# Fixing the order of all engines by hand in a four-layer graph attention kernel

## The chip, the core and the metric

The kernel runs on one core of a Trainium2 chip. The core has a matrix engine (TensorE, PE in the profile), a vector engine (VectorE, DVE), an engine for activation functions (ScalarE, ACT), a general engine that here issues the indirect transfers (GpSimd, POOL), an engine that only issues transfers (SyncE, SP), and 16 DMA engines. Each engine works through a list of instructions of its own, and semaphores order the lists among each other. The metric is the time of one execution on the device in microseconds (us); smaller is better.

## The reference

A graph of 3327 nodes with 512 features goes through four attention layers, each with a layer norm and a ReLU ahead of it and a residual around it. The adjacency is sparse: a node has itself and some 16 neighbours. Cut to layer 1 and the frame:

```python
def _L1_gnn_ref(H, A, W, a_l, a_r):
    mask = A + jnp.eye(n, dtype=A.dtype) > 0
    Wh = (H @ W).reshape(n, N_HEADS, D_K)
    sl = jnp.einsum('nhd,hd->nh', Wh, a_l)
    sr = jnp.einsum('nhd,hd->nh', Wh, a_r)
    e = jax.nn.leaky_relu(sl[:, :, None] + sr.T[None, :, :], negative_slope=NEG_SLOPE)
    e = jnp.where(mask[:, None, :], e, -jnp.inf)
    alpha = jnp.nan_to_num(jax.nn.softmax(e, axis=2), nan=0.0)
    out = jnp.einsum('nhm,mhd->nhd', alpha, Wh).reshape(n, OUT_DIM)
    return jax.nn.elu(out)
...
# --- layer 1 (adj_preln) ---
h = jnp.maximum(_layernorm(x, axis=-1), 0.0)
x = x + _L1_gnn_ref(h, adj, L1_gnn_W, L1_gnn_a_l, L1_gnn_a_r)
```

The layers have 8, 4, 1 and 8 heads; layers 1 and 2 end in an ELU, layers 0 and 3 don't. Everything is float32.

## The kernel before

A first stage (the first 416 us of the profile) turns the adjacency into lists of neighbours and projects the input for layer 0. It also sorts the nodes by their number of neighbours, so that each of 26 tiles of 128 nodes has its own cap, from 36 neighbours in tile 0 down to 11 in tile 25, 467 in all. The change leaves this stage as it is.

Then four layers run over the tiles. A table in HBM holds one row of 528 numbers per node: 512 projected features and 16 attention terms. For a tile, POOL gathers the rows of its nodes' neighbours, one indirect transfer of 128 rows per neighbour position, into buffers of four rows each (a group; there are 10 buffers):

```python
CAPS = [36, 25, 23, 22, 21, 21, 20, 20, 19, 19, 18, 18, 17, 17, 17, 16, 16, 15, 15, 15, 14, 14, 13, 13, 12, 11]
GROUP = 4
...
def fetch(l, t):
    groups = []
    for k0 in range(0, CAPS[t], GROUP):
        g = gpool.tile([P, GROUP, ROW], F32, name="g")
        n = min(GROUP, CAPS[t] - k0)
        for q in range(n):
            if l > 0 and k0 + q == 0:
                nc.sync.dma_start(g[:, 0, :], own_d[l % 2][t])
            else:
                gather(g[:, q, :], tabs[l % 2], idx[:, t, k0 + q:k0 + q + 1])
        groups.append((k0, n, g))
        if k0 == GROUP:
            scatter()
    return groups

def scatter():
    while waiting:
        dst, t, rows = waiting.pop(0)
        nc.gpsimd.indirect_dma_start(out=dst, out_offset=bass.IndirectOffsetOnAxis(ap=ids[t], axis=0),
                                     in_=rows, in_offset=None)
```

`attend` computes the weights of each group (z, a leaky step, an Exp), multiplies the rows by them and sums them in PSUM with matmuls by the identity; then it divides by the sum of the weights, applies the ELU where there is one and adds the residual. A float32 matmul shows as two records in the trace.

```python
def attend(l, t, groups):
    ...
    nc.vector.tensor_copy(s[:, :H], groups[0][2][:, 0, F:F + H])
    ...
    for k0, n, g in groups:
        z = small.tile([P, GROUP, 8], F32, name="z")
        nc.vector.tensor_tensor(z[:, :n, :H], g[:, :n, F + 8:F + 8 + H],
                                s[:, :H].unsqueeze(1).to_broadcast([P, n, H]), OP.add)
        nc.vector.scalar_tensor_tensor(z[:, :n, :H], z[:, :n, :H], SLOPE, z[:, :n, :H], OP.mult, OP.max)
        w = wt[:, k0:k0 + n, :H]
        nc.scalar.activation(w, z[:, :n, :H], AF.Exp)
        if H == 1:
            for q in range(n):
                nc.scalar.activation(g[:, q, :F], g[:, q, :F], AF.Copy, scale=wt[:, k0 + q, 0:1])
        else:
            for q in range(n):
                v = g[:, q, :F].rearrange("p (h d) -> p h d", h=H)
                nc.vector.tensor_tensor(v, v, wt[:, k0 + q, :H].unsqueeze(2).to_broadcast([P, H, D]), OP.mult)
        for q in range(n):
            nc.tensor.matmul(po, ident, g[:, q, :F], start=(k0 + q == 0), stop=(k0 + q == K - 1))
    ... # den: sum of the weights, floor, reciprocal
    nc.vector.tensor_tensor(y.rearrange("p (h d) -> p h d", h=H), po.rearrange("p (h d) -> p h d", h=H),
                            den[:, :H].unsqueeze(2).to_broadcast([P, H, D]), OP.mult)
    if ELU[l]:
        elu(y)
    nc.vector.tensor_add(xs[t], xs[t], y)
```

`finish` norms the tile (bn_stats, bn_aggr, nine small steps for the reciprocal root, then xn), and `projected` transposes xn, applies the ReLU, multiplies by the next layer's weights and copies the row v out of PSUM. The row is scattered into the next layer's table by POOL.

```python
def projected(nc, W, xn, ident, ps_t, ps_v, work):
    ...
    for k in range(KC):
        nc.tensor.transpose(pt[:, k, :], xn[:, k * P:(k + 1) * P], ident)
    hT = work.tile([P, KC, P], F32, name="hT")
    nc.scalar.activation(hT, pt, AF.Relu)
    pv = ps_v.tile([P, 2, BANK], F32, name="pv")
    for s in range(2):
        for k in range(KC):
            nc.tensor.matmul(pv[:, s, :HF + H], hT[:, k, :], W.w[:, k, s, :HF + H],
                             start=(k == 0), stop=(k == KC - 1))
    v = work.tile([P, ROW], F32, name="v", bufs=3)
    nc.scalar.activation(v[:, :F].rearrange("p (s n) -> p s n", s=2), pv[:, :, :HF], AF.Copy)
    ...
    nc.vector.tensor_copy(v[:, F:ROW].rearrange("p (s h) -> p s h", s=2)[:, :, :H], pv[:, :, HF:HF + H])
    return v
```

The layers' loop. Only POOL's list is in program order; the lists of the other engines are laid out by the scheduler of the language when the kernel is built.

```python
ctx.enter_context(tc.manual_schedule(engines={mybir.EngineType.Pool}))
for l in range(NL):
    W = Weights(nc, wpool, work, l + 1, ws, avs) if l + 1 < NL else None
    if l == 0:
        gather(xs[0], x, ids[0])
    ahead = fetch(l, 0)
    for t in range(NT):
        if l == 0 and t + 1 < NT:
            gather(xs[t + 1], x, ids[t + 1])
        now, ahead = ahead, fetch(l, t + 1) if t + 1 < NT else None
        attend(l, t, now)
        finish(l, t, W)
    scatter()
```

Of the kernel before, what the change touches and what calls it, by code (L numbers as in the profile page):

```python
# [398 lines left out]
def normed(nc, xt, small, work, half=None):  # L399


    st = small.tile([P, nc.vector.BN_STATS_DIM], F32, name="st")
    nc.vector.bn_stats(st, xt)
    mv = small.tile([P, nc.vector.BN_AGGR_DIM], F32, name="mv")
    nc.vector.bn_aggr(mv, st)
    ve = small.tile([P, 1], F32, name="ve")
    nc.vector.tensor_scalar_add(ve, mv[:, 1:2], EPS)  # L407
    rstd = small.tile([P, 1], F32, name="rstd")
    if half is not None:
        nc.gpsimd.tensor_tensor(rstd, ve, half, OP.pow)  # L410
    else:
        hv = small.tile([P, 1], F32, name="hv")
        nc.vector.tensor_scalar(hv, ve, -0.5, None, OP.mult)
        nc.vector.tensor_scalar(rstd.bitcast(I32), ve.bitcast(I32), -0.5, float(0x5F3759DF), OP.mult, OP.add)
        for _ in range(3):
            q = small.tile([P, 1], F32, name="q")
            nc.vector.tensor_scalar(q, rstd, rstd, hv, OP.mult, OP.mult)
            r2 = small.tile([P, 1], F32, name="rstd")
            nc.vector.tensor_scalar(r2, q, 1.5, rstd, OP.add, OP.mult)
            rstd = r2  # L420
    xn = work.tile([P, xt.shape[1]], F32, name="xn")
    nc.vector.tensor_scalar(xn, xt, mv[:, 0:1], rstd, OP.subtract, OP.mult)  # L422
    return xn


def projected(nc, W, xn, ident, ps_t, ps_v, work):

    F = xn.shape[1]
    HF, KC, H = F // 2, F // P, W.H
    pt = ps_t.tile([P, KC, P], F32, name="pt")  # L430
    for k in range(KC):
        nc.tensor.transpose(pt[:, k, :], xn[:, k * P:(k + 1) * P], ident)  # L432
    hT = work.tile([P, KC, P], F32, name="hT")
    nc.scalar.activation(hT, pt, AF.Relu)  # L434
    pv = ps_v.tile([P, 2, BANK], F32, name="pv")
    for s in range(2):
        for k in range(KC):
# [4 lines that stand above are left out]
    if H < 8:  # L442
        nc.vector.memset(v[:, F:ROW], 0.0)
    nc.vector.tensor_copy(v[:, F:ROW].rearrange("p (s h) -> p s h", s=2)[:, :, :H], pv[:, :, HF:HF + H])  # L444
    return v
# [3 lines left out]
def tile_gat_stack(ctx: ExitStack, tc: tile.TileContext, x, adj, adjT, ws, avs, out):  # L449
# [33 lines left out]
    with ExitStack() as c1:  # L483
# [26 lines left out]
        for t in range(NT):  # L510
            a = apool.tile([P, NP], I32, name="a")
            nc.sync.dma_start(a, adj[t * P:(t + 1) * P, :])
            key = apool.tile([P, NP], F32, name="key")
            nc.vector.scalar_tensor_tensor(key, a, 0.0, keys, OP.is_gt, OP.mult, accum_out=total[:, t:t + 1])  # L514
            dg = key[:, t * P:(t + 1) * P]
            nc.vector.tensor_add(dg, dg, boost)
            cand = small.tile([P, SEGS * 8], F32, name="cand")
            for g in range(SEGS):
                nc.vector.max(cand[:, g * 8:(g + 1) * 8], key[:, g * SEG:(g + 1) * SEG])  # L519
            for r in range(0, KMAX, 8):  # L520
                nc.vector.max(top[:, t, r:r + 8], cand)
# [4 lines left out]
            v = projected(nc, W, normed(nc, xt, small, work, half), ident, ps_t, ps_v, work)  # L526
            nc.sync.dma_start(tabs_v[0][t][t * P:(t + 1) * P, :], v)


# [94 lines left out]
def tile_gat_lists(ctx: ExitStack, tc: tile.TileContext, x, ws, avs, out, ident, half, idx, tabs, tabs_v):  # L624
# [37 lines left out]
                else:  # L662
                    gather(g[:, q, :], tabs[l % 2], idx[:, t, k0 + q:k0 + q + 1])
            groups.append((k0, n, g))
            if k0 == GROUP:
                scatter()
        return groups

# [3 lines left out]
            nc.gpsimd.indirect_dma_start(out=dst, out_offset=bass.IndirectOffsetOnAxis(ap=ids[t], axis=0),  # L672
                                         in_=rows, in_offset=None)

    def elu(y):

        neg = work.tile([P, F], F32, name="neg", bufs=1)
        nc.vector.tensor_scalar_min(neg, y, 0.0)
        th = work.tile([P, F], F32, name="th", bufs=1)
        nc.scalar.activation(th, neg, AF.Tanh, scale=0.5)  # L680
        nc.scalar.activation(neg, neg, AF.Exp)
        nc.vector.scalar_tensor_tensor(th, neg, 1.0, th, OP.add, OP.mult)
        nc.vector.scalar_tensor_tensor(y, y, 0.0, th, OP.max, OP.add)

    def attend(l, t, groups):
        H, D, K = HEADS[l], F // HEADS[l], CAPS[t]
        s = small.tile([P, 8], F32, name="s")
        nc.vector.tensor_copy(s[:, :H], groups[0][2][:, 0, F:F + H])
        wt = spool.tile([P, KMAX, 8], F32, name="wt")
        po = ps_o.tile([P, BANK], F32, name="po")  # L690
        for k0, n, g in groups:
            z = small.tile([P, GROUP, 8], F32, name="z")
            nc.vector.tensor_tensor(z[:, :n, :H], g[:, :n, F + 8:F + 8 + H],  # L693
                                    s[:, :H].unsqueeze(1).to_broadcast([P, n, H]), OP.add)
            nc.vector.scalar_tensor_tensor(z[:, :n, :H], z[:, :n, :H], SLOPE, z[:, :n, :H], OP.mult, OP.max)  # L695
            w = wt[:, k0:k0 + n, :H]
            nc.scalar.activation(w, z[:, :n, :H], AF.Exp)  # L697
            if H == 1:
                for q in range(n):
                    nc.scalar.activation(g[:, q, :F], g[:, q, :F], AF.Copy, scale=wt[:, k0 + q, 0:1])  # L700
            else:
                for q in range(n):
                    v = g[:, q, :F].rearrange("p (h d) -> p h d", h=H)
                    nc.vector.tensor_tensor(v, v, wt[:, k0 + q, :H].unsqueeze(2).to_broadcast([P, H, D]), OP.mult)  # L704
            for q in range(n):
                nc.tensor.matmul(po, ident, g[:, q, :F], start=(k0 + q == 0), stop=(k0 + q == K - 1))  # L706
        den = small.tile([P, 8], F32, name="den")
        nc.vector.tensor_reduce(den[:, :H], wt[:, :K, :H].rearrange("p k h -> p h k"), AX.X, OP.add)  # L708
        nc.vector.tensor_scalar_max(den[:, :H], den[:, :H], TINY)
        nc.vector.reciprocal(den[:, :H], den[:, :H])  # L710
        y = work.tile([P, F], F32, name="y")
        nc.vector.tensor_tensor(y.rearrange("p (h d) -> p h d", h=H), po.rearrange("p (h d) -> p h d", h=H),  # L712
                                den[:, :H].unsqueeze(2).to_broadcast([P, H, D]), OP.mult)
        if ELU[l]:
            elu(y)
        nc.vector.tensor_add(xs[t], xs[t], y)  # L716

    def finish(l, t, W):
        if W is None:
            waiting.append((out_v[t], t, xs[t]))  # L720
            return
        v = projected(nc, W, normed(nc, xs[t], small, work), ident, ps_t, ps_v, work)
        nc.sync.dma_start(own_d[(l + 1) % 2][t], v)
        waiting.append((tabs_v[(l + 1) % 2][t], t, v))

    out_v = dram_disjoint_views(out, NT)
    ctx.enter_context(tc.manual_schedule(engines={mybir.EngineType.Pool}))
    for l in range(NL):
        W = Weights(nc, wpool, work, l + 1, ws, avs) if l + 1 < NL else None
        if l == 0:  # L730
            gather(xs[0], x, ids[0])
        ahead = fetch(l, 0)
        for t in range(NT):
            if l == 0 and t + 1 < NT:
                gather(xs[t + 1], x, ids[t + 1])
            now, ahead = ahead, fetch(l, t + 1) if t + 1 < NT else None
            attend(l, t, now)
            finish(l, t, W)
        scatter()


# [38 lines left out]
```

## Time and profile before

| | |
|---|---|
| time, median of 3 | 3412.91 us (3411.35 to 3419.31) |
| span of the profiled execution | 3598.4 us |
| PE busy | 2458.3 us, 68% |
| DVE busy | 1895.9 us, 53% |
| ACT busy | 585.1 us, 16% |
| POOL busy | 1989.1 us, 55% |
| gathers g<-tab (L647, POOL) | 1790, mean 999 ns |
| sums po<-g,ident (L706, PE) | 3736 records, mean 652 ns |
| products g<-g,wt (L704, DVE; L700, ACT in layer 2) | 1401 of mean 689 ns; 467 of mean 710 ns |
| mean DMA rate | 175 GB/s |

The profiled execution is longer than the timed ones; stages and waits are read from the profile, the result from the times. A line of a group names line, engine, operation and tiles; then come the busy time and the mean of one, and after the bar the idle time of the engine just before these instructions, with what ended it. A line of waits names who waited for whom, with the total, the number of times and the longest. A line of a timeline has start, duration, engine, line, operation, tiles and shapes, and in brackets the idle time ahead of it and what ended it. PEclk is the share of the TensorE clock that was granted.

### The profile page before, as it was taken

The numbers are of one execution on the slowest core, as the hardware profiler recorded it, in microseconds if no ns is written. First come the engines' busy times: TensorE is split into PE (matmuls) and PEld (weight loads), VectorE is DVE, ScalarE is ACT, GpSimd is POOL, SyncE is SP. The second block draws the span as 40 slices with busy tenths as digits, with TensorE's granted clock in tenths as the row PEclk, the third lists the DMA queues.
The fourth block names the chain that finished last, engine by engine and source line by source line (L and its number), as shares of the span: only waits on it lengthen the run. The fifth ranks groups of instructions, "written<-read, shape, count | busy, mean of one in ns | idle before, by whom it ended". The sixth has DMA issues, their size and how long they took to land. (4 is left out here: it accounts for less than half of the span.)

```text
span 3598.4 us, 24474 instructions
## 1 busy us (share of the span) xinstructions
PE 2458.3 (68%) x5830; PEld 1217.5 (34%) x5830; DVE 1895.9 (53%) x5329; ACT 585.1 (16%) x1291; POOL 1989.1 (55%) x2025
## 2 busy tenths in 40 slices
PE   3564076777777657777776757677787857767677
PEld 2443033433334323333333323334343422322222
DVE  8999255555555536556655621222223345555555
ACT  0010000000000001011111134444454400000000
POOL 0002566666666365666655454555555456766666
PEclk8777588888888779889889877788988887879879
DMA  5552466666666475666665465566666556766666
GB/s 198 180 197 90 115 175 172 188 184 181 183 179 179 138 196 165 181 179 189 175 177 163 135 173 156 170 185 172 185 179 186 164 164 185 202 189 196 196 179 180
DMA packets 197001, 628.12 MB, mean 175 GB/s; under 512 B 38482, under 2 KB 42994, under 8 KB 193524
## 3 DMA queue, kind: packets, MB, share of 16 engines
q0 software_dynamic: 154432, 519.29, 51.2%
q1 hardware_dynamic: 33300, 94.07, 8.1%
q10 hardware_dynamic: 9120, 13.11, 1.1%
q8 instruction: 53, 0.87, 0.1%
q14 instruction: 96, 0.79, 0.1%
HBM read 569.76 MB, written 56.57 MB: 174 GB/s over the span
## 5 line engine op out<-in xcount | busy, mean ns | idle before, releaser
L706 PE MATMUL po<-g,ident 128*128 128x512 f32 x3736 | 1877.5, 652 | 547.7 <-issue 239.4
L647 POOL DMA_INDIRECT g<-tab,idx x1790 | 1788.8, 999 | 595.1 <-issue 510.2
L706 PEld LDWEIGHTS po<-g,ident 128*128 128x128 f32 x3736 | 750.0, 207 | 1541.3 <-issue 1078.4
L704 DVE TENSOR_TENSOR g<-g,wt 128x512 f32<-128x512 f32 x1401 | 903.6, 689 | 95.4 <-issue 63.7
L693 DVE TENSOR_TENSOR z<-g,s 128x32 f32<-128x32 f32 (+5 forms) x508 | 91.7, 182 | 969.9 <-DMA g<-tab,idx 903.2
L438 PE MATMUL pv<-w,hT 128*128 128x264 f32 (+2 forms) x1664 | 514.6, 476 | 76.2 <-ACT hT L434 56.8
L438 PEld LDWEIGHTS pv<-w,hT 128*128 128x128 f32 x1664 | 401.0, 245 | 239.5 <-ACT hT L434 91.1
L697 ACT ACTIVATE wt<-z 128x32 f32<-128x32 f32 (+5 forms) x508 | 107.2, 217 | 2122.8 <-DVE z L695 969.9
L432 PE MATMUL pt<-ident,xn 128*128 128x128 f32 x416 | 98.9, 382 | 447.5 <-DVE xn L422 232.5
L672 POOL DMA_INDIRECT tab<-v,idx x78 | 85.7, 1098 | 569.6 <-DVE v L444 501.7
L700 ACT ACTIVATE g<-g,wt 128x512 f32<-128x512 f32 x467 | 302.5, 710 | 3.8
L432 PEld LDWEIGHTS pt<-ident,xn 128*128 128x128 f32 x416 | 65.8, 192 | 528.4 <-issue 243.3
L410 POOL TENSOR_TENSOR rstd<-ve,half 128x1 f32<-128x1 f32 x26 | 14.3, 549 | 309.8 <-DVE ve L407 302.0
L712 DVE TENSOR_TENSOR y<-po,den 128x512 f32<-128x512 f32 x104 | 71.2, 685 | 173.6 <-PE po L706 126.9
L695 DVE SCALAR_TENSOR_TENSOR z<-z 128x32 f32<-128x32 f32 (+5 forms) x508 | 88.0, 178 | 96.1 <-remote 43.6
L519 DVE MAX8 cand<-key 128x8 f32<-128x208 f32 x416 | 129.1, 373 | 0.0
L434 ACT ACTIVATE hT<-pt 128x512 f32<-128x512 f32 x104 | 61.7, 594 | 306.9 <-PE pt L432 136.3
L441 ACT ACTIVATE v<-pv 128x512 f32<-128x512 f32 x104 | 61.4, 590 | 303.1 <-PE pv L438 254.0
L444 DVE COPY v<-pv 128x16 f32<-128x16 f32 (+2 forms) x104 | 17.8, 171 | 147.0 <-ACT v L441 147.0
L514 DVE SCALAR_TENSOR_TENSOR key<-a,keys 128x3328 f32<-128x3328 int32 x26 | 94.0, 3616 | 0.0
L716 DVE TENSOR_TENSOR x<-x,y 128x512 f32<-128x512 f32 x104 | 71.7, 690 | 3.0 <-DVE den L708 1.2
L672 POOL DMA_INDIRECT out<-x,idx x26 | 28.4, 1093 | 77.2 <-DVE x L716 42.0
(83 smaller groups left out, 794.3 us busy)
## 6 DMA issues: line engine op xcount, KB each, us to landing
a<-in_adj SPq DMA_DIRECT2D x26, 1664.0 KB
g<-tab,idx POOLq DMA_INDIRECT x1790
own<-v SPq DMA_DIRECT2D x78, 264.0 KB
g<-own SPq DMA_DIRECT2D x78, 264.0 KB
tab<-v SPq DMA_DIRECT2D x26, 264.0 KB
xt<-in_x ACTq DMA_DIRECT2D x26, 256.0 KB
w<-in_w ACTq DMA_DIRECT2D x8, 512.0 KB
av<-in_a ACTq DMA_DIRECT2D x8, 256.0 KB
```

Source lines behind the costliest of these rows:

```text
L432: nc.tensor.transpose(pt[:, k, :], xn[:, k * P:(k + 1) * P], ident)
L438: nc.tensor.matmul(pv[:, s, :HF + H], hT[:, k, :], W.w[:, k, s, :HF + H], start=(k == 0), stop=(k == KC - 1))
L514: nc.vector.scalar_tensor_tensor(key, a, 0.0, keys, OP.is_gt, OP.mult, accum_out=total[:, t:t + 1])
L519: nc.vector.max(cand[:, g * 8:(g + 1) * 8], key[:, g * SEG:(g + 1) * SEG])
L647: nc.gpsimd.indirect_dma_start(out=out_, out_offset=None, in_=table, in_offset=bass.IndirectOffsetOnAxis(ap=which, axis=0))
L672: nc.gpsimd.indirect_dma_start(out=dst, out_offset=bass.IndirectOffsetOnAxis(ap=ids[t], axis=0), in_=rows, in_offset=None)
L693: nc.vector.tensor_tensor(z[:, :n, :H], g[:, :n, F + 8:F + 8 + H], s[:, :H].unsqueeze(1).to_broadcast([P, n, H]), OP.add)
L695: nc.vector.scalar_tensor_tensor(z[:, :n, :H], z[:, :n, :H], SLOPE, z[:, :n, :H], OP.mult, OP.max)
L697: nc.scalar.activation(w, z[:, :n, :H], AF.Exp)
L700: nc.scalar.activation(g[:, q, :F], g[:, q, :F], AF.Copy, scale=wt[:, k0 + q, 0:1])
L704: nc.vector.tensor_tensor(v, v, wt[:, k0 + q, :H].unsqueeze(2).to_broadcast([P, H, D]), OP.mult)
L706: nc.tensor.matmul(po, ident, g[:, q, :F], start=(k0 + q == 0), stop=(k0 + q == K - 1))
```

## The change

The lists of PE, DVE and ACT are put in program order too, and the program is rewritten into pieces, so that the order can be chosen: as soon as a tile's last sums are traced, its end follows (division, residual, norm), and its transposes (`turn`) and its projection (`project`) are set behind the next tile's groups 0 and 1. In the layers with an ELU the residual and norm (`added`) come behind group 0, the transposes behind group 1 and the projection behind group 2. Besides:

- the scatter stands behind the third group of gathers in place of the second;
- in layers with several heads the fourth row of each group is weighted by ScalarE, one instruction a head, in place of VectorE;
- in the layer with one head the division is done by ScalarE;
- the ELU's lower clamp is a Relu on ScalarE;
- the weights of a layer are prepared in the middle of the layer but one before it.

The purpose is that the end of a tile no longer stands behind work of the next tile that waits for gathers. The core of the diff:

```diff
             groups.append((k0, n, g))
-            if k0 == GROUP:
+            if k0 == 2 * GROUP:
                 scatter()
...
+        def group(self, i):
...
             for q in range(n):
+                if H == 1 or q == 3:
+                    for h in range(H):
+                        v = g[:, q, h * D:(h + 1) * D]
+                        nc.scalar.activation(v, v, AF.Copy, scale=wt[:, k0 + q, h:h + 1])
+                else:
                     v = g[:, q, :F].rearrange("p (h d) -> p h d", h=H)
                     nc.vector.tensor_tensor(v, v, wt[:, k0 + q, :H].unsqueeze(2).to_broadcast([P, H, D]), OP.mult)
...
+        def weighted(self):
...
+            if H == 1:
+                nc.scalar.activation(self.y, po, AF.Copy, scale=den[:, 0:1])
+            else:
+                nc.vector.tensor_tensor(self.y.rearrange("p (h d) -> p h d", h=H), ...
+            if ELU[self.l]:
+                nc.scalar.activation(neg, self.y, AF.Relu, scale=-1.0)
+                nc.scalar.activation(self.th, neg, AF.Tanh, scale=-0.5)
+                nc.scalar.activation(self.ex, neg, AF.Exp, scale=-1.0)
+
+        def added(self):
+            y, xt = self.y, xs[self.t]
+            if ELU[self.l]:
+                nc.vector.scalar_tensor_tensor(self.th, self.ex, 1.0, self.th, OP.add, OP.mult)
+                nc.vector.scalar_tensor_tensor(y, y, 0.0, self.th, OP.max, OP.add)
+            nc.vector.tensor_add(xt, xt, y)
+            if self.W is None:
+                waiting.append((out_v[self.t], self.t, xt))
+            else:
+                self.xn = normed(nc, xt, small, work)
...
-    ctx.enter_context(tc.manual_schedule(engines={mybir.EngineType.Pool}))
+    ctx.enter_context(tc.manual_schedule(engines={mybir.EngineType.Pool, mybir.EngineType.PE,
+                                                  mybir.EngineType.DVE, mybir.EngineType.Activation}))
+    following = Weights(nc, wpool, work, 1, ws, avs)
...
+        late = 1 if ELU[l] else 0
+        todo = {}
+        ahead = Tile(l, 0, W)
         for t in range(NT):
...
+            now, ahead = ahead, Tile(l, t + 1, W) if t + 1 < NT else None
+            if t == NT // 2 and l + 2 < NL:
+                following = Weights(nc, wpool, work, l + 2, ws, avs)
+            now.start()
+            for i in range(len(now.groups)):
+                now.group(i)
+                for piece in todo.pop(i, []):
+                    piece()
+            now.weighted()
+            if late:
+                todo = {0: [now.added], 1: [now.turn], 2: [now.project]}
+            else:
+                now.added()
+                todo = {0: [now.turn], 1: [now.project]}
```

`Tile(l, t, W)` calls `fetch`, `start` copies s, `turn` is the first half of the old `projected` and `project` the second, with the store of v and its entry in `waiting`.

More of the change, by code (lines that the diff above doesn't have):

```diff
@@ L423, in normed, with turned @@
     return xn
-def projected(nc, W, xn, ident, ps_t, ps_v, work):
-    F = xn.shape[1]
-    HF, KC, H = F // 2, F // P, W.H
+def turned(nc, xn, ident, ps_t, work):
+    KC = xn.shape[1] // P
     pt = ps_t.tile([P, KC, P], F32, name="pt")
@@ L434, in projected @@
     nc.scalar.activation(hT, pt, AF.Relu)
+    return hT
+def projected(nc, W, hT, ps_v, work):
+    KC, H = hT.shape[1], W.H
+    F = KC * P
+    HF = F // 2
     pv = ps_v.tile([P, 2, BANK], F32, name="pv")
@@ L525, in tile_gat_stack @@
             nc.scalar.dma_start(xt, x[t * P:(t + 1) * P, :])
-            v = projected(nc, W, normed(nc, xt, small, work, half), ident, ps_t, ps_v, work)
+            v = projected(nc, W, turned(nc, normed(nc, xt, small, work, half), ident, ps_t, work), ps_v, work)
             nc.sync.dma_start(tabs_v[0][t][t * P:(t + 1) * P, :], v)
@@ L673, in scatter @@
                                          in_=rows, in_offset=None)
[L675 to L691, printed above, removed]
+    class Tile:
+        def __init__(self, l, t, W):
+            self.l, self.t, self.W = l, t, W
+            self.groups = fetch(l, t)
+        def start(self):
+            H = HEADS[self.l]
+            self.s = small.tile([P, 8], F32, name="s")
+            nc.vector.tensor_copy(self.s[:, :H], self.groups[0][2][:, 0, F:F + H])
+            self.wt = spool.tile([P, KMAX, 8], F32, name="wt")
+            self.po = ps_o.tile([P, BANK], F32, name="po")
+        def group(self, i):
+            H, K, wt = HEADS[self.l], CAPS[self.t], self.wt
+            D = F // H
+            k0, n, g = self.groups[i]
@@ L692, in attend @@
             z = small.tile([P, GROUP, 8], F32, name="z")
             nc.vector.tensor_tensor(z[:, :n, :H], g[:, :n, F + 8:F + 8 + H],
-                                    s[:, :H].unsqueeze(1).to_broadcast([P, n, H]), OP.add)
+                                    self.s[:, :H].unsqueeze(1).to_broadcast([P, n, H]), OP.add)
             nc.vector.scalar_tensor_tensor(z[:, :n, :H], z[:, :n, :H], SLOPE, z[:, :n, :H], OP.mult, OP.max)
-            w = wt[:, k0:k0 + n, :H]
-            nc.scalar.activation(w, z[:, :n, :H], AF.Exp)
@@ L698, in attend @@
[L698 to L702, printed above, removed]
+            nc.scalar.activation(wt[:, k0:k0 + n, :H], z[:, :n, :H], AF.Exp)
+            for q in range(n):
+                if H == 1 or q == 3:
[3 more added lines that the diff above has]
+                else:
@@ L705, in attend @@
             for q in range(n):
[L706 to L724, printed above, removed]
+                nc.tensor.matmul(self.po, ident, g[:, q, :F], start=(k0 + q == 0), stop=(k0 + q == K - 1))
@@ new lines, in weighted @@
+        def weighted(self):
+            H, K, po = HEADS[self.l], CAPS[self.t], self.po
+            D = F // H
+            den = small.tile([P, 8], F32, name="den")
+            nc.vector.tensor_reduce(den[:, :H], self.wt[:, :K, :H].rearrange("p k h -> p h k"), AX.X, OP.add)
+            nc.vector.tensor_scalar_max(den[:, :H], den[:, :H], TINY)
+            nc.vector.reciprocal(den[:, :H], den[:, :H])
+            self.y = work.tile([P, F], F32, name="y")
+            if H == 1:
+                nc.scalar.activation(self.y, po, AF.Copy, scale=den[:, 0:1])
+            else:
+                nc.vector.tensor_tensor(self.y.rearrange("p (h d) -> p h d", h=H),
+                                        po.rearrange("p (h d) -> p h d", h=H),
+                                        den[:, :H].unsqueeze(2).to_broadcast([P, H, D]), OP.mult)
+            if ELU[self.l]:
+                neg = work.tile([P, F], F32, name="neg", bufs=1)
+                nc.scalar.activation(neg, self.y, AF.Relu, scale=-1.0)
+                self.th = work.tile([P, F], F32, name="th", bufs=1)
+                nc.scalar.activation(self.th, neg, AF.Tanh, scale=-0.5)
+                self.ex = work.tile([P, F], F32, name="ex", bufs=1)
+                nc.scalar.activation(self.ex, neg, AF.Exp, scale=-1.0)
@@ new lines, in added, with turn @@
+        def added(self):
[8 more added lines that the diff above has]
+                self.xn = normed(nc, xt, small, work)
+        def turn(self):
+            if self.W is not None:
+                self.hT = turned(nc, self.xn, ident, ps_t, work)
@@ L726, in tile_gat_lists, with project @@
+        def project(self):
+            if self.W is not None:
+                v = projected(nc, self.W, self.hT, ps_v, work)
+                nc.sync.dma_start(own_d[(self.l + 1) % 2][self.t], v)
+                waiting.append((tabs_v[(self.l + 1) % 2][self.t], self.t, v))
     out_v = dram_disjoint_views(out, NT)
-    ctx.enter_context(tc.manual_schedule(engines={mybir.EngineType.Pool}))
+    ctx.enter_context(tc.manual_schedule(engines={mybir.EngineType.Pool, mybir.EngineType.PE,
+                                                  mybir.EngineType.DVE, mybir.EngineType.Activation}))
@@ L728, in tile_gat_lists @@
+    following = Weights(nc, wpool, work, 1, ws, avs)
     for l in range(NL):
-        W = Weights(nc, wpool, work, l + 1, ws, avs) if l + 1 < NL else None
+        W, following = following, None
         if l == 0:
             gather(xs[0], x, ids[0])
-        ahead = fetch(l, 0)
+        late = 1 if ELU[l] else 0
+        todo = {}
+        ahead = Tile(l, 0, W)
         for t in range(NT):
@@ L735, in tile_gat_lists @@
                 gather(xs[t + 1], x, ids[t + 1])
-            now, ahead = ahead, fetch(l, t + 1) if t + 1 < NT else None
-            attend(l, t, now)
-            finish(l, t, W)
+            now, ahead = ahead, Tile(l, t + 1, W) if t + 1 < NT else None
[12 more added lines that the diff above has]
+                todo = {0: [now.turn], 1: [now.project]}
+        for i in sorted(todo):
+            for piece in todo[i]:
+                piece()
         scatter()
```

## The prediction

> **What bounds the kernel now.** I read the table by stage first, with the stages cut at the last scatter of each layer (416 us is the first gather). Its columns are busy time and count by engine, then PEclk, DMA share and GB/s.
>
> ```profile
> 416.00:1257.00 841.00, 595.80 (x1454) 305.55 (x1454) 467.57 (x1269) 56.51 (x179) 535.99 (x518) 0.81 0.63 178
> 1257.00:2090.00 833.00, 597.62 (x1454) 289.41 (x1454) 490.54 (x1336) 86.14 (x231) 477.01 (x468) 0.86 0.60 171
> 2090.00:2900.00 810.00, 593.66 (x1454) 298.49 (x1454) 214.56 (x831) 380.32 (x698) 451.74 (x467) 0.84 0.61 174
> 2900.00:3594.00 694.00, 488.51 (x934) 190.78 (x934) 383.30 (x876) 28.51 (x127) 464.06 (x467) 0.84 0.67 192
> ```
>
> No engine is full in any layer and the DMA stands at 0.60 to 0.67, so a chain of waits sets the pace. The four layers are 3178 us of the 3598; the change leaves the rest alone. Next the waits of POOL, which issues every gather (engine, tile and line; releaser; us, times, longest):
>
> ```profile
> POOL tab L672 <- DVE v L444: 501.7, 65, 21.3
> POOL out L672 <- DVE x L716: 42.0, 6, 9.7
> ```
>
> The timeline of POOL shows what such a wait is. The scatter of a projected tile stands in POOL's queue between gathers, and everything behind it stops:
>
> ```profile
> 1009.84 1.08 POOL L647 DMA_INDIRECT g<-tab,idx  x1 [0.30 <-issue]
> 1011.23 0.95 POOL L647 DMA_INDIRECT g<-tab,idx  x1 [0.30 <-issue]
> 1016.83 1.20 POOL L672 DMA_INDIRECT tab<-v,idx  x1 [4.66 <-DVE v L444]
> 1018.33 0.96 POOL L647 DMA_INDIRECT g<-tab,idx  x1 [0.30 <-issue]
> ```
>
> Adding POOL's idle ahead of scatters by layer gives 149, 207, 212 and 73 us. Without it, a layer costs POOL its pitch, busy 0.96 to 1.03 plus 0.30 of issue: 519 transfers in layer 0 make 690 us, 467 in each other layer 585 to 612. That is the prize: some 640 us of POOL waiting. The question is what the other engines need per tile.
>
> VectorE shows why v is late, in its timeline at the end of layer 0: the statistics of a tile that is ready stand behind a z that waits for gathers (first three lines), while the last tile runs undisturbed (the others).
>
> ```profile
> 1224.05 0.69 DVE L403 BATCH_NORM_STATS2 st<-x 128x6 f32<-128x512 f32 x1
> 1228.28 0.18 DVE L693 TENSOR_TENSOR z<-g,s 128x24 f32<-128x24 f32 x1 [3.54 <-DMA g<-tab,idx]
> 1228.38 0.18 DVE L405 BATCH_NORM_AGGREGATE mv<-st 128x2 f32<-128x6 f32 x1
> ...
> 1241.57 0.69 DVE L712 TENSOR_TENSOR y<-po,den 128x512 f32<-128x512 f32 x1 [0.92 <-PE po L706]
> 1242.30 0.69 DVE L716 TENSOR_TENSOR x<-x,y 128x512 f32<-128x512 f32 x1
> 1243.03 0.69 DVE L403 BATCH_NORM_STATS2 st<-x 128x6 f32<-128x512 f32 x1
> ...
> 1246.09 0.55 DVE L422 TENSOR_SCALAR xn<-x,mv,rstd 128x512 f32<-128x512 f32 x1
> 1246.55 1.28 DVE L393 TENSOR_TENSOR prod<-w,av 128x512 f32<-128x512 f32 x2
> ```
>
> From y's start to the next free slot behind xn are 1246.55 - 1241.57 = **4.98 us**. Before, this chain is spread among the next tile's weighting; it takes 10 to 16 us there, but TensorE has sums to do meanwhile.
>
> **What the Trainium skill says.** "TensorE: Matmul & The Clock Gate", in the section on the 16 sub-arrays (Architectural detail), says that the queues of ScalarE and VectorE are strict first in, first out. The lines above agree: the aggregate starts 0.10 us after the z that stood ahead of it. So an order fixed by hand makes each wait in the list a wait for all that follows. The same page, Part 1 ("What's actually happening"), gives the clock two states, half and full, judged over windows of some 3.4 us. The trace agrees: only 0.5 and 1.0 occur, in stretches of multiples of 3.41 us, and PEclk of 0.81 to 0.86 means that 28 to 38% of the time ran at half. "ScalarE: Activation LUTs" ("What ACT_TABLE_LOAD costs") gives an ACTIVATE 186 ns + 0.833 ns per element, 93 more for a pointer operand, 93 of overlap back to back. The 128x512 copy with a pointer scale works out at 706; the trace has 710.
>
> **Part 1: POOL.** The scatter queued in tile t+1's gathers now belongs to tile t-2, and stands behind 12 gathers in place of 8. Its v is ready a whole tile earlier, so POOL waits no more for it, only for free gather buffers (10 groups). The 149 + 207 + 212 us end as scatter waits, and gathers lie ready ahead of VectorE.
>
> **Part 2: TensorE's own work.** In the timeline 28 sums take 12.18 us, 0.43 each at full clock; a neighbour is two of them, 0.86 us, 467 neighbours a layer: **401 us**. A projection is 16 matmuls at 0.22, 3.5 us, and 4 transposes at 0.21, 0.86 us.
>
> **Part 3: where TensorE now stands still.** The step times between starts, from the timelines: last sum's slot to y 0.2; s, z and the leaky step to Exp 0.2 + 0.2 + 0.23; Exp to the first product 0.26; product to sum 0.75. Together a restart is 1.64 us.
> - Layer 0. VectorE does y, x, statistics and xn at once, before the next tile's s: 0.2 + 4.98 + 1.64 = 6.8 us without a sum.
> - The turn follows group 0. ScalarE's list has hT, which waits for the transposes, ahead of group 1's Exp. Last transpose to hT 0.46, hT to Exp 0.50, then 0.26 + 0.75, less the transpose's own 0.21: 1.8 us idle.
> - The projection follows group 1. ScalarE's v and VectorE's copy of v's tail stand ahead of group 2: 0.42 + 0.61 + 0.1 + 0.2 + 0.22 + 0.26 + 0.75 - 0.22 = 2.3 us idle.
> - Fixed per tile: 6.8 + 0.9 + 1.8 + 3.5 + 2.3 = 15.3 us. Layer 0: 401 + 26 x 15.3 = 798 us.
> - Layer 1 (ELU). y is 0.72, then Relu, Tanh and Exp (0.6 + 0.65 + 0.54) stand on ScalarE ahead of the next tile's Exp: idle 3.75. After group 0's products VectorE does two ELU steps, x and the statistics, 5.6 us, ahead of group 1's z: 8.9 us from the first product to group 1's first sum, against 0.75 + 3.43 of summing: 4.7 idle. With the common 8.5: 16.9 per tile, 401 + 439 = 840 us.
> - Layer 2 (one head, weights applied by ScalarE). y is on ScalarE too: idle 3.75; group 1 again waits for the end of x and the statistics: 2.7 idle. 14.9 per tile, 401 + 387 = 788 us.
> - Layer 3 has no projection: idle 3.3 per tile, and 0.86 per neighbour is below POOL's 1.29. POOL sets it: 467 x 1.285 = 600, with start and end 630 us.
>
> ScalarE's eight 128x64 products of the fourth row cost an estimated 0.24 us each by the page named above, 1.9 us, done before TensorE reaches that row: nothing on the path. The three products left to VectorE save it 0.6 us a group, where it isn't the one waited for.
>
> **Part 4: the clock.** A pause of 3.8 to 6.8 us fills most of a window, and group 0 then runs at half: 3.4 us more at most, partly hidden in layer 1 by the 4.7 us stall; the 2.3 us stall drops it again now and then. Before, 28 to 38% of 32 us a tile ran at half, 9 to 12 us, some six tenths of it busy, which lost 2.7 to 3.7 us. I take 3.5, 3.0 and 2.7 in the three layers: 239 us.
>
> **Part 5: the rest.** Weights are made in mid-layer, twice: 8 products and 8 sums at 0.7, and a load that waits for the buffer of the first half, 15 us each, 30. At three layer changes the last projection, scatter and first gathers stand alone, some 13 us more each, and the start fills in 10: 50 us.
>
> **Sum:** 798 + 840 + 788 + 630 + 239 + 50 + 30 = 3375 us against 3178: +197. Without the profiler the kernel takes 3413, not 3598; I keep the difference: 3610. The loss by the clock is the softest term, so I go a little below: **3590 us**.
>
> **Rivals.** (a) *POOL becomes the bound*: the waits vanish and layers fall to 690 + 612 + 585 + 600, with 70 for changes: 3413 - 620 = about 2790 us. For it speak the 501.7 us and that these are the longest waits of the gathering engine; against it that the fixed 15 to 17 us per tile exceed what POOL's 1.29 per neighbour leaves above TensorE's 0.86, except for the first tile of 36 neighbours. (b) *The chain is as I drew it, but the clock holds*, since data lies ready and sums run densely between stalls: 239 us less, 3375 - 239 = 3136, so about 3370, no change. (c) *The half clock spreads*: each stall drops it, group 0 and group 1 both run at half, up to 3 us a tile more in three layers, 234 us: 3820. (d) *The profiler slows gathers more than sums*: then the kernel before gains more without it than the one after, worth up to 100 us upward.
>
> **Range and chances.** (b) and the sum mark the lower half, parts of (c) and (d) the upper: 3380 to 3780. Faster by over 2% needs the stalls of part 3 to be hidden by something I don't see: 0.17. Within 2%: 0.15. Slower: 0.68.
>
> **What would show it.** Right: POOL's scatter waits near zero and in their place waits for sums to free buffers; VectorE's 903 us of waiting for gathers gone in the first three layers, replaced by waits for po and for ScalarE; ScalarE waiting for pt and pv with Exp behind; a TensorE pause of some 6.8 us per tile of layer 0; PEclk about 0.8; layer 3 down to about 630 while layers 0 to 2 grow. Wrong: layers 0 to 2 below 750, or POOL busy at its pitch throughout.

## The result and the profile after

The change makes the kernel slower: 3743.43 us (median of 4) against 3412.26 us, a ratio of 1.0966 with a 95% interval of 1.0933 to 1.1000. That is 331 us more.

The same table by stage for the changed kernel, cut again at the last scatter of each layer:

```profile
412.00:1345.00 933.00, 622.74 (x1454) 300.59 (x1454) 439.22 (x1167) 273.29 (x1035) 513.77 (x519) 0.83 0.57 161
1345.00:2279.00 934.00, 629.34 (x1454) 296.79 (x1454) 453.85 (x1202) 235.90 (x685) 463.63 (x467) 0.87 0.54 152
2279.00:3119.00 840.00, 603.94 (x1454) 287.69 (x1454) 195.97 (x774) 413.70 (x750) 450.73 (x468) 0.89 0.59 168
3119.00:3744.00 625.00, 471.07 (x934) 191.56 (x934) 333.22 (x769) 245.11 (x983) 469.48 (x468) 0.90 0.76 213
```

Against the first profile layers 0 and 1 have grown by 92 and 101 us, layer 2 by 30, and the DMA share of layer 1 fell from 0.60 to 0.54: no engine is full, and for the most part the core waits more. TensorE's row of one tile of layer 0, in the timeline, names the waits:

```profile
1001.17 0.60 PE L431 MATMUL pt<-ident,xn 128*128 128x128 f32 x4
1003.30 3.70 PE L715 MATMUL po<-g,ident 128*128 128x512 f32 x8 [1.53 <-DVE g L713]
1006.84 3.67 PE L445 MATMUL pv<-w,hT 128*128 128x260 f32 x16
1012.89 8.83 PE L715 MATMUL po<-g,ident 128*128 128x512 f32 x16 [2.38 <-DVE g L713]
1028.49 6.51 PE L715 MATMUL po<-g,ident 128*128 128x512 f32 x8 [6.77 <-DVE g L713]
1034.84 0.60 PE L431 MATMUL pt<-ident,xn 128*128 128x128 f32 x4
```

In the brackets stand the three pauses of a tile: 1.53 us behind the turn, 2.38 behind the projection, 6.77 behind the last sums. The group after the long pause takes 6.51 us for its eight records, where eight take 3.70 in the second line: most of it ran at half clock. All three pauses end with a product of VectorE, and ScalarE's Exp stands ahead of that product. What the Exp has to wait for differs. Behind the turn it stands behind hT in ScalarE's list, behind the projection behind v; behind the last sums it waits for VectorE, which first works through the tile's end. ScalarE's, POOL's and VectorE's rows show it in the same stretch:

```profile
1001.81 0.60 ACT L433 ACTIVATE hT<-pt 128x512 f32<-128x512 f32 x1 [5.25 <-PE pt L431]
1002.30 0.22 ACT L705 ACTIVATE wt<-z 128x32 f32<-128x32 f32 x1
...
1010.55 0.60 ACT L448 ACTIVATE v<-pv 128x512 f32<-128x512 f32 x1 [5.97 <-PE pv L445]
1011.88 0.23 ACT L705 ACTIVATE wt<-z 128x32 f32<-128x32 f32 x1 [0.73 <-DVE z L704]
...
1035.28 0.95 POOL L654 DMA_INDIRECT g<-tab,idx  x1 [7.00 <-PE po L715]
...
1021.75 0.69 DVE L729 TENSOR_TENSOR y<-po,den 128x512 f32<-128x512 f32 x1 [4.46 <-PE po L715]
...
1026.73 0.27 DVE L692 COPY s<-g 128x8 f32<-128x8 f32 x1
```

ScalarE sat 5.25 us until the transposes were done, with the Exp right behind hT in its list, and 5.97 us until the projection was done, with v ahead of the next Exp. VectorE needs 4.98 us from y to the next tile's s (1026.73 - 1021.75). POOL now waits for sums to free a buffer: in this stretch gathers are not what is short.

### The profile page after: what moved, and what is told of

The parts are those of the page before. It is cut to its first block, busy times and chain, and to the rows that moved or that the text cites. A ratio compares the mean times of both kernels' runs of the same rounds, so it can differ in the third digit from the quotient of the medians.

```text
span 3747.7 us, 27283 instructions
## 1 busy us (share of the span) xinstructions
PE 2507.2 (67%) x5830; PEld 1207.5 (32%) x5830; DVE 1762.4 (47%) x4930; ACT 1201.6 (32%) x3509; POOL 1957.1 (52%) x2025
## 5 line engine op out<-in xcount | busy, mean ns | idle before, releaser
L715 PE MATMUL po<-g,ident 128*128 128x512 f32 x3736 | 2008.0, 694 | 982.4 <-DVE g L713 662.0
L654 POOL DMA_INDIRECT g<-tab,idx x1790 | 1764.5, 986 | 924.2 <-issue 474.6
L715 PEld LDWEIGHTS po<-g,ident 128*128 128x128 f32 x3736 | 794.1, 221 | 2118.2 <-DVE g L713 917.3
L710 ACT ACTIVATE g<-g,wt 128x64 f32<-128x64 f32 (+2 forms) x2607 | 869.1, 411 | 15.4 <-ACT wt L705 0.4
L713 DVE TENSOR_TENSOR g<-g,wt 128x512 f32<-128x512 f32 x1080 | 685.3, 688 | 366.4 <-ACT wt L705 366.4
L445 PE MATMUL pv<-w,hT 128*128 128x264 f32 (+2 forms) x1664 | 447.5, 429 | 21.8 <-ACT hT L433 21.8
L445 PEld LDWEIGHTS pv<-w,hT 128*128 128x128 f32 x1664 | 356.1, 216 | 130.5 <-ACT hT L433 31.9
L431 PE MATMUL pt<-ident,xn 128*128 128x128 f32 x416 | 72.0, 301 | 166.3 <-DVE xn L422 151.3
L745 DVE SCALAR_TENSOR_TENSOR th<-ex,th 128x512 f32<-128x512 f32 x52 | 36.1, 695 | 151.4 <-ACT ex L739 151.4
L735 ACT ACTIVATE neg<-y 128x512 f32<-128x512 f32 x52 | 32.7, 629 | 140.6 <-DVE y L729 139.8
```

The costliest lines, as they stand in the source:

```text
L654: nc.gpsimd.indirect_dma_start(out=out_, out_offset=None, in_=table, in_offset=bass.IndirectOffsetOnAxis(ap=which, axis=0))
L710: nc.scalar.activation(v, v, AF.Copy, scale=wt[:, k0 + q, h:h + 1])
L715: nc.tensor.matmul(self.po, ident, g[:, q, :F], start=(k0 + q == 0), stop=(k0 + q == K - 1))
```

## The experiments

The runs are told in the order of the questions.

### Was the profile of before typical?

`before_again` is the kernel before without an edit.

> The kernel before, unchanged, profiled once more: its profile on hand spans 3598 us though its times are 3411 to 3419. If the profiler stretches this kernel (gathers or their landing), the span is near 3600 again. If that one execution was just long, the span is near 3415, and then the stage lengths of before are some 6% shorter than those the prediction used, and the loss of the change by layer is larger than the two profiles show.

It took 3417.13 us and its profile spans 3415.4. So the profiler does not stretch this kernel; the execution that the first profile shows was a long one. It also has a mark of its own: ScalarE's copy v starts more than 1 us after its matmuls have ended and ScalarE is free in 13 of 104 cases, and in none of before_again. What held it there is not known. The stages of before_again:

```profile
414.00:1226.00 812.00, 582.85 (x1454) 301.75 (x1454) 466.01 (x1268) 56.51 (x179) 534.63 (x519) 0.84 0.65 185
1226.00:2011.00 785.00, 591.20 (x1454) 287.65 (x1454) 490.04 (x1336) 85.37 (x231) 477.90 (x468) 0.89 0.64 181
2011.00:2777.00 766.00, 572.07 (x1454) 289.41 (x1454) 215.35 (x832) 380.34 (x698) 452.01 (x468) 0.87 0.65 184
2777.00:3411.00 634.00, 476.50 (x934) 186.33 (x934) 384.76 (x876) 28.53 (x127) 474.18 (x467) 0.91 0.74 210
```

The layers are 812, 785, 766 and 634 us, 2997 in all, in place of 841, 833, 810 and 694. The loss by layer is thus 121, 149 and 74 us, and 9 us gained in layer 3: 335 together, the measured 331. Of the 344 us lost in the first three layers TensorE is busy for 110 (1746 to 1856 us, the first busy column) and stands still for the other 234.

### Is it the order, or the other parts of the change?

`scheduler_order` is the changed kernel with one line undone:

```diff
-    ctx.enter_context(tc.manual_schedule(engines={mybir.EngineType.Pool, mybir.EngineType.PE,
-                                                  mybir.EngineType.DVE, mybir.EngineType.Activation}))
+    ctx.enter_context(tc.manual_schedule(engines={mybir.EngineType.Pool}))
```

> The changed kernel with only POOL's order fixed; all its other parts (fourth row on ScalarE, division and clamp on ScalarE, scatter behind the third group, weights in mid-layer) stay. Stall theory (the fixed order of PE, DVE and ACT costs the time): close to before or faster, 3200 to 3420 us. Rival (the other parts cost it: eight small products on ScalarE, the weights in mid-layer): near the changed kernel, 3650 to 3750.

3323.58 us, a ratio of 0.9744 (0.9713 to 0.9775) to before. All the parts but the order together are a gain of 84 us against the 3407 us of before, timed beside it; this order by hand alone costs 3743 - 3324 = some 420 us. The rival falls.

`scatter_later_only` takes one of the other parts alone, on the kernel before:

```diff
-            if k0 == GROUP:
+            if k0 == 2 * GROUP:
                 scatter()
```

> The kernel before with only the scatter moved behind the third group of gathers. If POOL's wait for v is what bounds the kernel before, twelve gathers lie ahead of the wait in place of eight, 5 us more for v to come: the wait of 5 to 8 us per tile shrinks or goes, up to 26 x 5 us in three layers, 3050 to 3250 us. If the wait only stands in for a slow v, nothing moves: 3400 +- 30.

3381.72 us, 0.9927 (0.9904 to 0.9950): under 1%, 25 us, far from what the first theory allowed. POOL's wait for v is still 412.9 us in its profile, where it is 428.9 in before_again. The move by itself doesn't free POOL. Why four more gathers ahead of the wait shorten it so little was not taken apart.

### Which of the pauses costs it?

For the next kernels a group was split into its weights and products (`front`) and its sums (`sums`), and the loop sets the fronts of later groups ahead; with AHEAD = 0 it would be the changed kernel.

```diff
+        fronts = [(ahead, i) for i in range(len(ahead.groups))]
...
             for i in range(len(now.groups)):
-                now.group(i)
+                while fronts and (done < j + AHEAD + 1) and (fronts[0][0] is now or fronts[0][0] is ahead):
+                    f, k = fronts.pop(0)
+                    f.front(k)
+                    done += 1
+                now.sums(i)
+                j += 1
                 for piece in todo.pop(i, []):
                     piece()
```

`ahead_inside_tile`: AHEAD = 1, but only fronts of the running tile (`fronts[0][0] is now`).

> The changed kernel with the weights and products of one next group set ahead of the sums, but only within a tile: the turn and the projection no longer hold up the next group's Exp; the pause at the tile's end stays. Stall theory, by its pieces: 1.5 and 2.4 us per tile go in three layers, 26 x 3.9 x 3 = 304 us, and in layer 1 and 2 the wait of group 1 for the added tile shrinks little; 3400 to 3470. If TensorE's pauses at turn and projection were hidden: 3700 and more.

3279.37 us, 0.9620 (0.9604 to 0.9636) of before. That is 464 us less than the changed kernel, more than the 304 that the two pauses were reckoned at. The stages of the first three layers:

```profile
413.00:1203.00 790.00, 574.47 (x1454) 288.81 (x1454) 439.33 (x1167) 273.35 (x1035) 512.82 (x518) 0.85 0.66 190
1203.00:1955.00 752.00, 572.18 (x1454) 281.74 (x1454) 453.12 (x1202) 235.93 (x685) 461.72 (x468) 0.90 0.66 189
1955.00:2652.00 697.00, 569.80 (x1454) 285.05 (x1454) 195.26 (x774) 412.66 (x750) 451.30 (x468) 0.90 0.70 202
```

By layer 143, 182 and 143 us went, 468 in all: TensorE stands still for 328 us less and is busy for 140 us less. The pauses behind turn and projection are gone but for 0.6 us behind the turn in layer 1 and two long waits in the middle of layers 1 and 2; the pause at the end of a tile stands as it was (median 6.67 us in layer 0, 3.5 in layers 1 and 2). The shorter busy time is in the main the clock: TensorE's busy time at half clock fell from 199 + 199 + 146 us to 127 + 100 + 113, and half of that difference, 102 us, is time; what the other 38 are was not taken apart.

`one_group_ahead`: AHEAD = 1 also across the tile's end.

> The same across the tile's end: group 0 of the next tile is weighted ahead of the end. Stall theory: the tile's end now overlaps one group's sums, 3.4 of the 6.8 us of layer 0 and about 3.5 of layers 1 and 2; 26 x 3.5 x 3 = 270 us less than inside the tile alone, 3150 to 3250, most of what two groups ahead bring (3174).

3180.12 us, 0.9327 (0.9311 to 0.9342): another 99 us. Expected were 270. The pause behind the last sums goes in layer 0, and in layers 1 and 2 some 30 pauses with a median of 1.3 us are left between sums; in its place TensorE waits ahead of the transposes for xn, a median of 2.91, 3.20 and 1.26 us per tile in the three layers.

`two_groups_ahead`: AHEAD = 2.

> The changed kernel, order fixed by hand in the same way, but weights and products of the next two groups (also of the next tile's) are set in the lists ahead of a group's sums, so ahead of a tile's end, its turn and its projection. Stall theory: TensorE's three pauses of 6.8, 1.5 and 2.4 us per tile go, TensorE needs some 20.8 us for a tile of 18, POOL 22.7 to 25.2, so POOL's pitch bounds: layers of about 700, 620, 600 and 620 us, 2950 to 3100 in all. Rival (fixed order as such, or the half clock, costs it): 3500 to 3750.

3174.25 us, 0.9317 (0.9297 to 0.9337): better than the kernel before and the changed one, and no different from one group ahead. The expectation of 2950 to 3100 was missed. Its stages, and what TensorE waits for most (the second block; 37.7 us is a wait of the first stage):

```profile
413.00:1125.00 712.00, 560.58 (x1454) 288.16 (x1454) 442.56 (x1167) 271.92 (x1035) 519.11 (x519) 0.90 0.74 211
1125.00:1877.00 752.00, 568.33 (x1454) 291.27 (x1454) 454.17 (x1202) 236.73 (x685) 475.28 (x468) 0.87 0.66 190
```

```profile
PE pt L432 <- DVE xn L423: 480.7, 100, 37.7
PE po L722 <- DVE g L716: 175.2, 91, 14.5
```

Layer 0 is at 712 us, near the 690 of POOL's pitch, with 0.74 of DMA. Layer 1, at 752, is far above the 620 expected. TensorE stands ahead of the transposes for a median of 4.7 us per tile in layer 0 and 5.0 in layer 1. The turn was left where the change put it, and may now come too early for xn, as sums no longer wait; that this holds layer 1 is argued, not shown.

`ahead_over_end_only`: as one group ahead, but inside a tile the order of the changed kernel.

```diff
-                while fronts and (done < j + AHEAD + 1) and ...
+                while fronts and (done < j + 1 + (AHEAD if i == len(now.groups) - 1 else 0)) and ...
```

> The changed kernel with only group 0 of the next tile weighted ahead of a tile's end; inside a tile the turn and the projection stand ahead of the next Exp as before. It parts the gain of one group ahead (563 us) into its two places. If the two pauses are independent: the tile's end alone brings 563 - 464 = 99 us, 3640. If group 0's sums just fill 3.4 us of the pause and shield less of what follows: 3.4 x 26 x 3 = 265 us, 3480; turn and projection then still cost their 3.9 us per tile.

3952.93 us, 1.1091 (1.1064 to 1.1118) of the kernel before. In this run and the three that follow, the kernel before, timed beside them, took 3565 and 3556 us in place of some 3410, so that only a ratio to before, and no time, can be read from them. Their profiles have the mark of the first profile of before: v starts over 1 us late in 16 to 47 of 104 cases (here one starts at 898.94 us, 6.4 us after its matmuls end at 892.53), and in the profiles of the other runs never. The ratio is no lower than the changed kernel's 1.0966, so no gain of the tile's end alone is to be seen, but the two were not timed beside each other. How the 563 us split if the end is freed first stays open.

`turn_one_group_later`, run a second time as `turn_later_again`: two groups ahead with

```diff
-                todo = {0: [now.added], 1: [now.turn], 2: [now.project]}
+                n = len(ahead.groups) if ahead is not None else 4
+                todo = {0: [now.added], 2: [now.turn]}
+                todo.setdefault(min(3, n - 1), []).append(now.project)
...
-                todo = {0: [now.turn], 1: [now.project]}
+                todo = {1: [now.turn], 2: [now.project]}
```

> Two groups ahead, and the turn and the projection one group later still (in the ELU layers the added tile after group 0, the turn after group 2). In two_groups_ahead TensorE waits 4.9, 5.1 and 3.4 us per tile ahead of the transposes for xn, 356 us in three layers. Stall theory: these go; POOL's pitch then bounds layers 0 to 2 at about 690, 620 and 600: 3030 to 3090. If POOL's waits for v take their place: 3150 to 3200.

> turn_one_group_later once more. In the call that held it every kernel was slower (the kernel before took 3565 in place of 3407 to 3412 us), so its 3437 us can't be set beside the 3174 of two_groups_ahead. Undisturbed: 3030 to 3100 if TensorE's wait for xn ahead of the transposes was the next bound; 3160 to 3200 if POOL's waits take its place.

3437.15 us, 0.9637 (0.9616 to 0.9659), and 3436.80 us, 0.9670 (0.9647 to 0.9694). The ratios are higher than that of two_groups_ahead (0.9317), but they belong to the runs just named and can't be held against it. Whether the later turn helps is not settled.

`turn_and_scatter_later` adds the edit of `scatter_one_tile_later` below.

> The same with the scatter held back by one more tile (5 buffers for v). Without effect on the changed kernel; where POOL is the bound its waits ahead of scatters (228 us in two_groups_ahead) count. 2990 to 3050 if they bound it, the same as turn_one_group_later within 15 us if not.

3462.79 us, 0.9723 (0.9694 to 0.9752): 26 us behind `turn_one_group_later`, timed beside it. Holding the scatter back does not help there.

### Does POOL's wait for v matter in the changed kernel?

POOL still waits 482 us ahead of scatters in the changed kernel. `scatter_one_tile_later`:

```diff
-        while waiting:
+        while len(waiting) > keep:
...
             if k0 == 2 * GROUP:
-                scatter()
+                scatter(keep=1)
...
-    v = work.tile([P, ROW], F32, name="v", bufs=3)
+    v = work.tile([P, ROW], F32, name="v", bufs=5)
```

> The changed kernel with the scatter held back by one more tile (5 buffers for v in place of 3), so that POOL finds v ready. POOL waits 482 us ahead of scatters in the changed kernel, against the prediction. Stall theory: POOL would wait for buffers in place of v, 3720 to 3760. Rival (POOL's wait for v bounds this kernel as it did the one before): 3450 to 3600.

3746.10 us, 1.0993 (1.0974 to 1.1011): no change. POOL's waits ahead of scatters fell to 270 us and came back as a wait for buffers, first line the changed kernel, second this one:

```profile
POOL g L654 <- PE po L715: 248.9, 144, 16.5
```

```profile
POOL g L654 <- PE po L715: 449.2, 179, 24.7
```

The rival falls: POOL has time in this kernel.

### What does the half clock cost?

`clock_fill` keeps TensorE running over the pause at the tile's end. The extra matmuls write a bank that nobody reads.

```diff
+            if W is not None:
+                junk = ps_j.tile([P, BANK], F32, name="junk")
+                for _ in range(4 if late else 7):
+                    nc.tensor.matmul(junk, ident, fill, start=True, stop=True)
             now.weighted()
```

> The changed kernel with idle matmuls put behind each tile's last sums (7 in layer 0, 4 in layers 1 and 2, 0.86 us each, their results unused), to keep TensorE's clock full over the pause. The pauses themselves stay. If the half clock costs what the prediction took (239 us in three layers, most of it after the tile's end): 120 to 240 us less, 3500 to 3620, PEclk above 0.9. If the half clock falls into time that TensorE waits anyway: 3700 to 3760.

3756.22 us, 1.1025 (1.1007 to 1.1043): nothing gained, as the second case expected, though the clock did rise (0.853 to 0.891 in the mean). By layer it is two things: layer 0 fell from 933 to 860 us, layers 1 and 2 grew from 934 to 963 and from 840 to 884:

```profile
412.00:1272.00 860.00, 706.73 (x1818) 340.91 (x1818) 439.29 (x1167) 273.34 (x1035) 510.08 (x519) 0.95 0.61 174
1272.00:2235.00 963.00, 709.34 (x1662) 334.45 (x1662) 453.30 (x1202) 235.95 (x685) 465.65 (x468) 0.88 0.52 148
2235.00:3119.00 884.00, 695.16 (x1662) 327.45 (x1662) 195.98 (x774) 413.78 (x750) 451.54 (x467) 0.91 0.56 159
```

In layer 1 the timeline shows why; first a tile of the changed kernel, then one of clock_fill:

```profile
1710.68 6.75 PE L715 MATMUL po<-g,ident 128*128 128x512 f32 x8 [3.50 <-DVE g L713]
1718.94 3.70 PE L715 MATMUL po<-g,ident 128*128 128x512 f32 x8 [1.51 <-DVE g L713]
```

```profile
1605.45 3.60 PE L791 MATMUL junk<-fill,ident 128*128 128x512 f32 x8
1609.08 3.70 PE L718 MATMUL po<-g,ident 128*128 128x512 f32 x8
1617.35 5.39 PE L718 MATMUL po<-g,ident 128*128 128x512 f32 x8 [4.57 <-DVE g L716]
```

Group 1 starts when VectorE's chain lets it, 11.8 us after the last sum in the first (1718.94 - 1710.68 + 3.50) and 11.9 in the second (1617.35 - 1605.45). With the clock kept full, group 0 is done in 3.70 us in place of 6.75, and TensorE then pauses 4.57 us in place of 1.51. Behind that longer pause group 1 takes 5.39 us in place of 3.70, and its time isn't hidden. In the changed kernel only some tiles of layer 1 go this way, in clock_fill nearly all.

So in layer 0, where sums follow the pause without another wait, the clock was worth time: TensorE's busy time at half clock fell from 199 to 52 us, and half of that difference, 73 us, is what the layer gained. In layer 1, where group 0 ran slow, the loss was hidden ahead of group 1. For layer 2 the trace shows a growth of the same kind (its second pause is mostly 2.5 us in place of 0.8 to 1.0), but the 44 us were not taken apart.

## Why the prediction was right, and where its size was off

It foresaw a slower kernel, and 3743 us lies in its range; the middle, 3590, was 153 us low.

**The pauses (part 3) were right to a few tenths.** Layer 0: 6.8, 1.8 and 2.3 us against a median of 6.68, 1.53 and 2.31 in the trace. Layer 1: 3.75 and 4.7 us with group 0 at full clock, measured 3.46 to 3.50 and then mostly 1.5 to 4.5, the less the longer group 0 ran at half. From the tile's last sum to group 1's first, 3.75 - 0.75 + 8.9 = 11.9 us by the working, it took 11.8. The eight small products of ScalarE, estimated at 1.9 us, took 2.02 us of a group in which nobody waits for them.

**The layers were right.** With the 50 and 30 us of part 5 spread over their layers, and the clock's 91, 78 and 70 us, the working gives 927, 946, 871 and 630 us, 3374 in all. The trace has 933, 934, 840 and 625: 3332. Layer 2 was 31 us too long in the working.

**The step that was mis-sized is the last one: "Without the profiler the kernel takes 3413, not 3598; I keep the difference".** The difference of 197 us was taken from the 3178 us of layers in the one long profile. Against the 2997 us of a typical execution the same sum of 3375 gives +378, or some 3790 us; with the measured sum of 3332 it is 335, near the 331 measured. So the same working on a typical profile would have given a middle above the range's upper end of 3780, and 47 us over the measured time; going from 3610 down to 3590 went the wrong way too. That the range held owes something to its width. Rival (d) named the right direction with the wrong reason and half the size: it was not that the profiler slows gathers, since before_again spans 3415 us with it.

**Layer 3's gain was that same error**: 694 us to 625 in the two profiles first compared, 634 to 625 against before_again. There POOL's pitch already bounded the kernel before: 474 us busy and 467 times 0.30 of issue are 614 of the 634 us.

**Part 1 was half wrong.** POOL's waits ahead of scatters did not end; they come to 482 us. In each layer the scatters of the first 13 or 14 tiles wait 0.3 us, as foreseen; those of the later ones, 5 to 30 us. From there on the tiles being gathered have four groups or fewer, so that with 10 buffers POOL runs up to two tiles ahead and comes upon the scatter before the tile's v, in spite of the further tile between. But it waits in time that it has, as `scatter_one_tile_later` shows. VectorE's waits for gathers fell as foreseen, from 903 us to 302, 107 of them in the first three layers.

**Part 4 was near in sum, but not all of it is time.** Predicted 239 us; half of the busy time at half clock is 100 + 100 + 73 = 273 us in the trace, of which `clock_fill` gave back the 73 us of layer 0 and nothing in layers 1 and 2. Rival (b), the clock that holds, did not come: PEclk is 0.83 to 0.89 in the three layers. Nor was it tried by `clock_fill`, where TensorE is still busy at half clock for 182 and 147 us of layers 1 and 2, against 199 and 146. Rival (c), 234 us more of half clock than the 239, did not come either.

**Rival (a), POOL as the bound, lost** for the change as it is: layers 0 to 2 take 933, 934 and 840 us. It shows what was left lying: with two groups' weights and products ahead layer 0 comes to 712 us, against the 690 of POOL's pitch.

## What to carry to other kernels

In a list kept in order by hand, ask of every instruction that waits what stands behind it: an end, a copy out of PSUM or an activation that waits for another engine belongs behind the next group's first steps, not ahead of them. Here that move turned 3743 us into 3279, and with one group ahead over the tile's end into 3180. The scheduler's order with the same other parts took 3324, so that of the gain over the kernel before, 3412, only what lies below 3324 is the order's. An end set at once behind its tile is worth little where its result, here v, is wanted only a tile later. And check that the profiled execution has the length of the timed ones before its stages serve as the base of a difference.

## What the runs showed of the hardware

Keeping TensorE busy with unused matmuls raised the mean granted clock from 0.853 to 0.891 and made the kernel no faster: layer 0 gained 73 us, and layers 1 and 2 lost 29 and 44. In layer 1 the first group after a pause ran in 3.70 in place of 6.75 us, and the longer pause ahead of the next group (4.57 in place of 1.51 us) took the gain and the clock with it. A half clock next to a wait is partly free.

In these traces the clock has a memory. It changes only at multiples of 3.41 us. Cut the four layers of the first profile of before into such windows, and take for each the share in which a matmul was running. After a window at full clock the next ran at half in all 109 cases with a share under 0.4, and stayed full in all 501 with one over 0.5. After a window at half clock the next was full in 117 of 121 cases with a share over 0.8, and in none of 175 below. Layers 0 to 2 of the changed kernel give the same: 130 of 130, 411 of 411, 137 of 141 and 0 of 80. By this count a pause of 1.5 us, which leaves 0.56 of a window, does not drop the clock by itself, one of 2.4 us (0.30) can (53 of the 137 drops in layers 0 to 2 of the changed kernel come without a pause over 2.5 us), and to win it back takes a window nearly full of sums.
